# Five counted node tiles instead of six in layer 2 of a two-layer graph network

## The chip, the core and the metric

The kernel runs on one core of a Trainium2 chip. The time is the device time of one execution in microseconds (us); 15 executions of the kernel before have a median of 1412.94 us (1409.12 to 1421.94). Engines: PE (TensorE, matrix products; PEld is its loading of weights), DVE (VectorE), ACT (ScalarE), POOL (GpSimd), SP (SyncE, which only issues transfers here).

## What is computed

A graph has 6250 nodes with 256 features (x) and 100,000 edges src to dst, sorted by dst. The destination is drawn as 6250 u² with u uniform, so nodes with a small number have far more edges than the others. Two layers each add to a node the rows of all its edges' sources and put the sum through two dense products; a residual and a layer norm follow.

```python
def _gin_agg(h, src, dst, eps, n_nodes):
    agg = jax.ops.segment_sum(h[src], dst, num_segments=n_nodes)
    return (1.0 + eps) * h + agg

h = _gin_agg(x, src, dst, eps1, n)
h = jax.nn.relu(h @ W1a + b1a)          # 256 -> 512
h = jax.nn.relu(h @ W1b + b1b)          # 512 -> 512
h = _gin_agg(h, src, dst, eps2, n)
h = jax.nn.relu(h @ W2a + b2a)          # 512 -> 512
out = h @ W2b + b2b                     # 512 -> 256
return _layernorm(x + out)
```

All values are float32.

## The kernel before

**Tiles and chunks.** The nodes lie in 49 tiles of 128 (the last has 106). The edges lie in 782 chunks of 128, in order of dst. There are two ways to sum the rows of the edges:

- *By gathering.* For each chunk, one indirect DMA that GpSimd issues (L270, in `gather`) fetches 128 rows of the table (x, 1 KB a row, in layer 1; h, 2 KB a row, in layer 2) into a buffer called early, in layer 2 early and late. A matmul with a 0/1 matrix `sel` (L1109) adds the rows up within 32 slots. Chunks are taken in groups of 1 to 5 chunks for each of four quarters of the array; at the end of a group the four partial sums are copied and split (L535, L536, L1133), put on their nodes by a matmul with `to` (L1158) and added to the accumulators `acc` of the two or three tiles that the group may reach (L1147).
- *By counts.* For the first, heavily used tiles, layer 1 builds a matrix of how many edges run from each source node to each node of the tile (L939, L942, L985, L955: 280 chunks). The sum is then a product of that matrix with the whole table, tile by tile of the table: 49 matmuls for one node tile in layer 1 (L885 with `both`), 98 in layer 2 (L885 with `upper` and with `xr`, the two halves of a float32 split). For this the table is loaded in 13 ranges of four tiles (`xr`, L823) and split (`cut`, L838). Layer 2 uses the same counts: layer 1 narrows them to 16 bits and stores them (L975, L978), layer 2 loads them (`ci`, L905) and widens them (`cf`, L906). The results are added to acc (L894).

`HEAVY = (7, 6)` (L24) says how many tiles go by counts: seven in layer 1, six in layer 2. `counted` (L65) turns it into the number of leading chunks that lie safely within so many tiles: NC = 280 in layer 1, NC2 = 264 in layer 2. `places` (L100) cuts the chunks beyond into groups, first those from NC2 to NC, then those from NC on; layer 1 takes the groups from `BEGIN` on, layer 2 all of them. So layer 1 gathers 502 chunks in 90 groups, layer 2 gathers 518 in 91.

**Order.** The order of the instructions is written out by the program itself (`manual_schedule`, L560). The main loop (L1093) walks the groups from the last node to the first. Four chunks make a piece; after the matmuls of a piece, the gather of the piece six further on is issued into the same buffer (L1117), so up to 24 chunks are under way:

```python
last_sum[upto] = mm
gathered[upto + PIECES] = gather(number, upto + PIECES, table, width, *places)
for c, b in pieces[number][upto][1]:
    tick()
    for q in both:
        q.pump()
```

With every chunk two queues of other work may put out instructions: `blockwise`, the dense products of those tile pairs whose sums are complete (`block`, L716: transposes L745, copies L754, first product L777, ReLU L786, second product L798, then `finish1` or `finish2`), and `beside`, the products by counts. `spread` (L125) works out how much of `beside` may go with each group, so that it lies where the dense work is thin; its work is proportional to the number of counted tiles (L1072), times a pace of 1.4 in layer 2.

**Blocks.** Tiles are put in pairs (L582 to L585): the counted ones from the front, the others from the back, and the tiles that the very last group reaches in pairs of their own. In layer 2 that makes [0,1], [2,3], [4,5], then [47,48] down to [7,8], and [6] alone at the end: 25 blocks. Each has an accumulator seeded with (1 + eps) times its own rows (L627, L634). Layer 2 begins when layer 1 has stored the last rows of h (L1189). Before its first group it seeds the counted blocks, puts out six steps of `beside`, and then loads the weights W2a and W2b (L511).

**Preparation.** Before either layer, DVE checks that the edges fit the plan (L359 to L491) and writes a flag; each engine branches on it (L1475, L1476). The first 22 gathers of layer 1 are issued ahead of that branch.

Of the kernel before, what the change touches and what calls it, by code (L numbers as in the profile page):

```python
# [20 lines left out]
SLOTS = 32  # L21
BURST = 4
PIECES = 6
HEAVY = (7, 6)  # L24

PASSES = [[6, 5], [4], [3, 2], [1, 0]]
RING = 4
# [37 lines left out]
def counted(N, E, tiles):  # L65

    def node(e):  # L70
        return N * min((e + deviation(e, E)) / E, 1.0) ** 2

    total = 0
    while (
        node((total + PARTS) * P) < tiles * P
        and span(N, E, (total + PARTS) * P, P, SIGMAS) <= W
    ):
        total += PARTS
    taken, at = [], 0
    for n in (8, 4, 2, 1):  # L80
        a = at
        while at + n <= total and span(N, E, (at + n) * P, n * P, SIGMAS) <= W:
            at += n
        if at > a:
            taken.append((a, at, n))
    return total, taken


def steps(N, E, taken, tiles):

    def reached(c):
        return N * min((c * P + deviation(c * P, E)) / E, 1.0) ** 2

    todo = sorted(((c, n) for a, b, n in taken for c in range(a, b, n)), reverse=True)
    return todo, [
        max(i for i, (c, n) in enumerate(todo) if reached(c + n) >= t * P) for t in range(tiles)
    ]


def places(N, E, c, chunks):  # L100

    def node(e, side):
        return N * min(max((e + side * deviation(e, E)) / E, 0.0), 1.0) ** 2

    groups, lo, hi = [], [], []  # L110
    while c < chunks:
        n = min(GRP, -(-(chunks - c) // PARTS) * PARTS)
        while n > PARTS and (
            span(N, E, (c + n) * P, n // PARTS * P, SPREAD, 1) > SLOTS
            or span(N, E, (c + n) * P, n * P, SPREAD, 1) > P
        ):
            n -= PARTS
        groups.append((c, n // PARTS))
        lo.append(int(node(c * P, -1)) // P)
        c += n  # L120
        hi.append(min(int(node(c * P, 1)), N - 1) // P)
    return groups, lo, hi
# [24 lines left out]
def tile_gin_residual_layernorm(  # L147
# [44 lines left out]
    NCH = -(-E // P)  # L192
    NC, taken = counted(N, E, HEAVY[0])
    STEPS, END = steps(N, E, taken, HEAVY[0])

    NC2 = counted(N, E, HEAVY[1])[0]
    assert NC2 <= NC and HEAVY[1] <= HEAVY[0]
    groups, lo, hi = (a + b for a, b in zip(places(N, E, NC2, NC), places(N, E, NC, NCH)))
    NG = len(groups)
    BEGIN = (next(g for g in range(NG) if groups[g][0] == NC), 0)  # L200
    assert lo[BEGIN[0]] >= HEAVY[1]
    NCP = groups[-1][0] + PARTS * groups[-1][1]
# [88 lines left out]
    with tc.tile_pool(name="prep", bufs=2) as prep, tc.tile_pool(  # L291
# [139 lines left out]
        for i in range(2):  # L431
            nc.vector.tensor_tensor(
                diff[:, i, full - NC2 :], diff[:, i, full - NC2 :], real, op=ALU.mult
            )
        bad = prep.tile([P, 8 + HEAVY[0]], F32, tag="bad", name="bad", bufs=1)
        nc.vector.memset(bad, 0.0)
# [1074 lines left out]
```

## Time and profile before

| | |
|---|---|
| median of 15 runs | 1412.94 us |
| the profiled execution | 1412.47 us |
| its span, first to last instruction | 1410.7 us |
| mean granted PE clock | 0.94 of full |
| busy: PE, PEld | 1206.9 us (86%), 724.2 us (51%) |
| busy: DVE, ACT, POOL | 902.2 us (64%), 487.2 us (35%), 1017.0 us (72%) |
| indirect DMAs, layer 1 and layer 2 | 502 and 518 |
| first and last gather issued, layer 1 | 9.67 and 671.37 us |
| first and last gather issued, layer 2 | 704.73 and 1368.86 us |
| HBM read and written | 279.57 MB, 28.83 MB |

A row of busy tenths divides the span into 40 slices of 35.3 us. A timeline row gives start, duration, engine and line, operation, output<-input, how many instructions were merged, and in brackets the idle time before with what ended it. A row of the waits gives the waiting engine and line, what it waited for, us in total, times, and the longest. A matmul in float32 stands in the trace as two records, so "L777 x32" is 16 matmuls of the program. Groups of PE give the time that the group fills and then the mean length of one record; where records overlap, the first is smaller than count times mean.

### The profile page before, as it was taken

What the parts mean: (1) busy time and instruction counts of PE and PEld (TensorE: products, weight loads), DVE (VectorE), ACT (ScalarE), POOL (GpSimd) and SP (SyncE); (2) the same over time, 40 slices, a digit from 0 to 9 for tenths busy, and PEclk for the clock granted to TensorE, in tenths of its full rate; (3) what the DMA queues carried; (4) which work ended last, traced back from release to release, by engine and by line L of the source; (5) the groups of instructions that cost most, each with busy time, mean ns of one, the idle gap of its engine ahead of it and who ended that gap; (6) DMA issues with size and microseconds to landing.
All of it is one profiled execution on the core that took longest, in us unless ns stands there. A gap on an engine that the chain in (4) does not pass through costs nothing. (4 is left out here: it accounts for less than half of the span.)

```text
span 1410.7 us, 18558 instructions
## 1 busy us (share of the span) xinstructions
PE 1206.9 (86%) x5929; PEld 724.2 (51%) x5929; DVE 902.2 (64%) x2267; ACT 487.2 (35%) x892; POOL 1017.0 (72%) x1034
## 2 busy tenths in 40 slices
PE   2589998889897896887845999999989999997977
PEld 1144564445453452553521666676666665663646
DVE  7998778899967667232126577868855654663323
ACT  0223652444344342561314224333423333321112
POOL 6777777777777777777077777777777777777760
PEclk9989999999999899898967899999999999998989
DMA  4645765666466555774398799898889889877761
GB/s 101 199 137 180 240 203 179 199 194 204 144 204 207 170 158 155 220 224 122 108 363 280 205 302 305 263 295 284 256 285 318 292 258 320 267 236 238 222 205 40
DMA packets 159242, 309.77 MB, mean 220 GB/s; under 512 B 25378, under 2 KB 89762, under 8 KB 159136
## 3 DMA queue, kind: packets, MB, share of 16 engines
q0 software_dynamic: 65536, 201.65, 46.5%
q1 hardware_dynamic: 73060, 82.55, 18.2%
q10 hardware_dynamic: 20540, 24.28, 5.1%
q8 instruction: 50, 0.82, 0.2%
q14 instruction: 56, 0.46, 0.1%
HBM read 279.57 MB, written 28.83 MB: 219 GB/s over the span
## 5 line engine op out<-in xcount | busy, mean ns | idle before, releaser
L270 POOL DMA_INDIRECT early<-in_x_dram,srcs x502 | 510.0, 1016 | 159.1 <-issue 132.6
L270 POOL DMA_INDIRECT early<-h,srcs x262 | 257.3, 982 | 112.3 <-issue 64.0
L270 POOL DMA_INDIRECT late<-h,srcs x256 | 247.2, 966 | 80.7 <-issue 64.9
L1147 DVE SCALAR_TENSOR_TENSOR acc<-bank,mask,acc 128x512 f32<-128x512 f32 (+1 forms) x421 | 231.6, 606 | 82.9 <-PE bank L1158 82.7
L1109 PE MATMUL bank<-early,sel 128*32 128x256 f32 (+1 forms) x1528 | 161.6, 499 | 85.8 <-DMA early<-in_x_dram,srcs 36.8
L798 PE MATMUL bank<-w1b_s,ht 128*128 128x512 f32 (+1 forms) x392 | 180.3, 606 | 3.4 <-ACT ht L786 2.9
L777 PE MATMUL bank<-zt,w2a_s 128*128 128x256 f32 (+2 forms) x800 | 181.7, 384 | 1.1 <-ACT zt L754 1.1
L777 PEld LDWEIGHTS bank<-zt,w2a_s 128*128 128x128 f32 x800 | 152.1, 195 | 38.5 <-issue 10.0
L1158 PE MATMUL bank<-split,to 128*128 128x512 f32 (+3 forms) x362 | 122.3, 445 | 25.8 <-ACT split L535 22.8
L885 PE MATMUL bank<-upper,cf 128*128 128x512 f32 (+1 forms) x294 | 125.3, 426 | 12.3 <-ACT cf L906 11.6
L955 DVE TENSOR_TENSOR at<-bank,at 128x490 f32 x173 | 115.0, 665 | 11.0 <-ACT cf L970 3.3
L1109 PEld LDWEIGHTS bank<-early,sel 128*32 128x32 f32 x1528 | 33.6, 112 | 171.0 <-issue 106.9
L798 PEld LDWEIGHTS bank<-w1b_s,ht 128*128 128x128 f32 (+1 forms) x392 | 73.8, 193 | 91.3 <-issue 75.8
L885 PE MATMUL bank<-both,cf 128*128 128x512 f32 (+1 forms) x343 | 111.1, 452 | 10.2 <-ACT ht L786 5.6
L786 ACT ACTIVATE ht<-bank,b2a_s 128x256 f32<-128x256 f32 (+2 forms) x100 | 41.5, 466 | 220.7 <-PE bank L777 216.3
L885 PE MATMUL bank<-xr,cf 128*128 128x512 f32 (+1 forms) x294 | 117.5, 400 | 0.0
L1158 PEld LDWEIGHTS bank<-split,to 128*128 128x128 f32 (+1 forms) x362 | 67.2, 202 | 82.1 <-ACT split L535 34.4
L536 DVE TENSOR_TENSOR both<-xr,both 128x1024 fp32r<-128x1024 f32 (+1 forms) x52 | 60.3, 1159 | 67.3 <-ACT both L535 67.1
L942 DVE TENSOR_SCALAR cb<-numbers,spot 128x490 f16<-128x490 f16 x280 | 103.1, 368 | 0.0
L985 PE MATMUL bank<-cb,ca 128*128 128x490 f16 x280 | 91.3, 395 | 11.7 <-DVE acc L1147 5.4
L654 DVE TENSOR_TENSOR sel<-iota,slot 128x256 f32<-128x256 f32 (+3 forms) x119 | 51.4, 432 | 77.3 <-PE bank L1109 76.4
L777 PE MATMUL bank<-zt,w1a_s 128*128 128x256 f32 (+2 forms) x416 | 96.1, 379 | 3.7 <-DVE at L955 2.6
(132 smaller groups left out, 1556.3 us busy)
## 6 DMA issues: line engine op xcount, KB each, us to landing
xr<-in_x_dram SPq DMA_DIRECT2D x48, 512.0 KB
h<-h1r ACTq DMA_DIRECT2D x48, 256.0 KB
xr<-h SPq DMA_DIRECT2D x12, 1024.0 KB
acc<-h SPq DMA_DIRECT2D x23, 512.0 KB
counts<-ci ACTq DMA_DIRECT2D x72, 128.0 KB
ci<-counts SPq DMA_DIRECT2D x72, 128.0 KB
early<-in_x_dram,srcs POOLq DMA_INDIRECT x502
r<-in_x_dram SPq DMA_DIRECT2D x23, 256.0 KB
```

The lines of the kernel that those rows point to most:

```text
L270: nc.gpsimd.indirect_dma_start(out=rows_[:, j, :], out_offset=None, in_=table, in_offset=bass.IndirectOffsetOnAxis(ap=srcs[:, c : c + 1], ...
L536: nc.vector.tensor_tensor(lower, of, upper, op=ALU.subtract)
L654: nc.vector.tensor_tensor(sel[:, :n, :], iota[:, :SLOTS].unsqueeze(1).to_broadcast([P, n, SLOTS]), slot[:, c0 : c0 + n].unsqueeze(2).to_br ...
L777: nc.tensor.matmul(ph[0][:, (f - o) * TILES * P : (f - o) * TILES * P + nb], wa[:, k, f * P : (f + 1) * P], zt[:, k, :nb], start=(k == 0), ...
L798: nc.tensor.matmul(po[0][:m], ht[:, f, i * P : i * P + m], wb[:, f, :], start=(f == 0), stop=(f == KH - 1),)
L885: nc.tensor.matmul(pm[0], cf[:m, j, :], of.rearrange("p a b -> p (a b)") if once else of, start=(opens and j == 0 and l == 0), stop=(close ...
L942: made = nc.vector.tensor_scalar(b, numbers, spot[:, c : c + 1], None, op0=ALU.is_equal)
L955: nc.vector.tensor_tensor(to, ap.rearrange("p (k w) -> p k w", w=W), to, op=ALU.add)
L985: mm = nc.tensor.matmul(pc[0], a, b, start=(i == 0), stop=(i == n - 1))
L1109: mm = nc.tensor.matmul(pm[b * SLOTS : (b + 1) * SLOTS], sel[:, c - c0, :], rows_[:, j, :], start=(c == parts[b][0]), stop=(c == parts[b][ ...
L1147: nc.vector.scalar_tensor_tensor(acc[t], ap[:, i * width : (i + 1) * width], mask[:, t - lo[g], g : g + 1], acc[t], op0=ALU.mult, op1=ALU.add,
L1158: nc.tensor.matmul(pu[0][:, i * width : (i + 1) * width], to[:used], split[:used, l, :], start=(once or l == 0), stop=(once or l == 1),)
```

## The change

```diff
--- before.py
+++ after.py
@@ -21,7 +21,7 @@
 SLOTS = 32
 BURST = 4
 PIECES = 6
-HEAVY = (7, 6)
+HEAVY = (7, 5)
 
 PASSES = [[6, 5], [4], [3, 2], [1, 0]]
 RING = 4
```

Layer 1 goes on counting seven tiles. It stores the counts of tiles 0 to 4 for layer 2, not those of tile 5 (L973). NC2 becomes 244, and the chunks 244 to 279 make three groups of 16, 16 and 4 chunks where 264 to 279 made one of 16. Layer 2 takes tiles 0 to 4 by counts and gathers 538 chunks in 93 groups; the last group reaches tile 5 alone. Its blocks are [0,1], [2,3], [4], then [47,48] down to [7,8], then [6] and [5], each alone: 26. The instructions of the main path that change in number (program's own instructions, a float32 matmul counted once):

| line | what | before | after |
|---|---|---|---|
| L270 | gathers of h | 518 | 538 |
| L1109 | matmuls on gathered rows, layer 2 | 518 | 538 |
| L1158 | matmuls with to, layer 2 | 182 | 186 |
| L1147 | additions of groups, layer 2 | 211 | 215 |
| L885 | products by counts, layer 2 | 588 | 490 |
| L894, L906, L905 | additions, widened counts, loads of counts, layer 2 | 78 | 65 |
| L975, L978 | narrowed and stored counts, layer 1 | 78 | 65 |
| L777 | first dense product, layer 2: two tiles wide, one tile wide | 368, 16 | 352, 48 |
| L381 to L396 | runs of equal groups in the preparation | 4 | 5 |

## The prediction

> **What bounds the kernel now.** I read four views in this order: the busy share by slice, the waits of each engine in the second layer, the instructions of GpSimd in order of time, and the chain that ended last. First the page: GpSimd's row of 40 slices, and its groups in layer 2.
>
> ```profile
> POOL 6777777777777777777077777777777777777760
> ...
> L270 POOL DMA_INDIRECT early<-h,srcs x262 | 257.3, 982 | 112.3 <-issue 64.0
> L270 POOL DMA_INDIRECT late<-h,srcs x256 | 247.2, 966 | 80.7 <-issue 64.9
> ```
>
> GpSimd shows the same 7 in nearly every slice. It issues one indirect DMA for each chunk of 128 edges, 262 + 256 = 518 of them in layer 2, about 0.97 us each. A steady seven tenths may still be an engine without a break, if the rest is its own pause between instructions. The waits of GpSimd from 700 us on say so:
>
> ```profile
> POOL late L270 <- issue: 64.9, 213, 0.3
> POOL early L270 <- issue: 64.0, 210, 0.3
> POOL early L270 <- DMA h<-h1r: 32.4, 1, 32.4
> ...
> POOL late L270 <- PE bank L1109: 4.8, 7, 3.0
> ```
>
> Columns: idle time in all, how often, longest. 423 idle times are "issue", none over 0.3 us: nothing outside held the engine. It waited 32.4 us once for the last rows of h between the layers, and 3.0 us once for a matmul that had to free a gather buffer. In order of time:
>
> ```profile
> 704.73 0.94 POOL L270 DMA_INDIRECT early<-h,srcs  x1 [32.41 <-DMA h<-h1r]
> ...
> 755.16 0.95 POOL L270 DMA_INDIRECT late<-h,srcs  x1 [3.02 <-PE bank L1109]
> ...
> 1368.86 0.94 POOL L270 DMA_INDIRECT late<-h,srcs  x1 [0.30 <-issue]
> ```
>
> So layer 2 is one unbroken row of gathers from 704.73 to 1368.86 us. TensorE looks as full in the middle, and this row of the busy time by windows is the strongest argument against GpSimd (us, then busy time and count of PE, PEld, DVE, ACT, POOL, then clock, DMA share, GB/s):
>
> ```profile
> 811.90:1235.50 423.60, 415.36 (x2131) 276.40 (x2123) 290.12 (x572) 149.64 (x289) 322.71 (x331) 0.98 0.88 287
> ```
>
> PE is busy 98% there. But had PE set the pace, it would have fallen behind until all 24 gather buffers were full, and GpSimd would have waited for it; in this window it did not, and by 1282 us PE stands waiting for gathers again ("DMA early<-h,srcs" and "late" hold L1109 for 40.3 us in all). The end is then the chain behind the last gathers:
>
> ```profile
> 1363.85 3.75 DMA early<-h,srcs
> ...
> 1367.74 1.07 PE bank L1109 x8
> ...
> 1398.00 3.57 PE bank L777 x32
> 1401.57 1.74 PE bank L798 x8
> ```
>
> **The change, part by part.** HEAVY[1] goes from 6 to 5. By the plan's own arithmetic the counted prefix of layer 2, NC2, falls from 264 chunks to 244, and the instruction lists of the two programs show the rest.
>
> *Twenty more gathers* (518 to 538), two more groups (91 to 93), on the engine that sets the pace. Over the whole layer the spacing is (1368.86 - 704.73 - 2.72)/517 = 1.279 us, the one long wait's excess taken out; the window above gives 423.6/331 = 1.280, and neighbours without any disturbance stand 1.25 apart. I take 20 x 1.28 = **+25.6 us**, ends 25.0 and 25.7 (664.13/517 = 1.285 x 20, the wait left in).
>
> [...]
>
> *One tile's products fewer in layer 2*: 49 + 49 matmuls less of L885.
>
> ```profile
> L885 PE MATMUL bank<-upper,cf 128*128 128x512 f32 x288 | 122.6, 426 | 12.3 <-ACT cf L906 11.6 <-DVE acc L894 0.8
> L885 PE MATMUL bank<-xr,cf 128*128 128x512 f32 x288 | 115.2, 400 | 0.0
> ```
>
> 48 x 0.426 + 48 x 0.400 + two short ones (0.83) = 40.5 us of PE. Added to PE: 20 chunks of L1109, which in layer 2 fill (73.4 + 72.5)/518 = 0.28 us a chunk (columns of the array overlap), 5.6 us; four L1158 at 65.0/180 = 0.36, 1.4 us. A pair of tiles becomes two single ones in the dense part ([4], [6], [5] stand alone where [4,5] and [7,8] with [6] stood): L777 in the chain takes 3.57 us for one tile, 7.17 for two, so about nothing. PE: 40.5 - 7.0 = 33.5 us less. On the path: **0**, because PE is covered by GpSimd's row. Without that cover it would be a gain of 33.5.
>
> *Other engines, layer 2*: ACT loses 13 conversions of counts (12 x 0.62 + 0.30 = 7.7 us), gains 2 x 0.59; DVE loses 13 additions of 0.685 (8.9 us), gains four of 0.74 and two of 0.68 and some masks, about 6. SP loses 13 loads of counts. DVE is busy 405 of the 690 us from 710 on, ACT 209: **0**, the same cover.
>
> *Layer 1*: tile 5's counts are no longer narrowed and stored, 13 casts (7.7 us) and 13 DMA issues on ACT less. The order of PE, SP and GpSimd there is unchanged. ACT is busy 257 of 610 us while gathers run back to back, so **0**; 7.7 us at most if ACT were the bound.
>
> *The preparation*: one more run of groups, some eight small DVE instructions, 1.1 us (the run at 17.36 to 18.5 us shows this sum). It delays the flag (33.62 us), behind which every engine's branch waits. GpSimd has 22 gathers in front of its branch and starts the 23rd at 37.56: 3.9 us of cover, less the branch. **0**; without cover +1.1.
>
> *The start of layer 2*: the 3.0 us wait at 755 comes from the first seeds of acc, which land at 746.66 behind some 3.6 MB of xr and weights; their order in SP's queue is the same but for one load of counts. ACT now has four casts of xr's second range (2.2 us) ahead of the seeds, in a stretch where it stands idle for 27.7 us. **0**, ends -2.7 and +3.
>
> *The tail.* Now: last gather issued at 1368.86, span ends 1410.7, 41.8 us, because the last L1109 stands in PE's order behind dense work that is itself late. In the changed order the last L1109 has one L798 for one tile (1.74) ahead of it, and GpSimd still 5 us to issue its piece, so it waits for its gather: 3.75 to landing (chain, above), 1.07 for its matmuls, then in PE's order L798 1.74, L777 7.17, L1158 0.47, L798 3.46, L745 0.44, the wait for zt 1.12, L777 3.57, L745 0.44, L798 1.74, L777 3.57, L798 1.74 (each from the chain), together 25.5; from the last matmul to the end 1410.7 - 1403.3 = 7.4. Sum 37.7: **-4.1**. But PE will have idled, and after waits of 4.7 and 2.4 us near 1350 an L777 pair took 8.95 instead of 7.07: +1.9. I take **-2.2**, ends -4.1 and +1.
>
> Sum: 25.6 - 2.2 = +23.4. The profiled execution took 1412.47 us (span 1410.7 and 1.8 around it), 0.5 below the median 1412.94. I predict a span of 1434.1 and a median of **1436.3 us**, +1.7%.
>
> **Rivals.**
> 1. *PE sets the pace of layer 2* (other side). For: 98% busy from 812 to 1236. Against: GpSimd's waits. It decides from the point where PE is more than 24 chunks (31 us) behind. Then the 33.5 us of PE go and the gathers hide: 1412.9 - 33.5 = 1379.
> 2. *The bytes set the pace.* For: a DMA share of 0.88 in that window. Against: GpSimd's waits for landings are all 0.6 us or less. 5.24 MB more of h, 1.6 MB less of counts, 3.6 MB at 265 GB/s (710 to 1400 us): +13.7, or 1427.
> 3. *PE, thinned out, runs slow, and the tail grows.* For: granted clock 0.86 and waits for gathers from 1270 to 1370 us, where PE has least to do. If the tail's 33 us of PE work lost a quarter more: 25.6 + 6 or so, 1444.
> 4. *The change does nothing*: excluded by the 20 further gathers in GpSimd's list.
>
> **How the numbers follow.** Forecast 0.83, rival 1 0.03, rival 2 0.05, rival 3 0.07, anything else near the old time 0.02. The forecast's own ends: 25.0 - 4.1 - 2.7 = +18.2 (1431) and 25.7 + 1 + 3 + 1.1 = +30.8, which all the worst cases together need; 1442 leaves out under 2 in 10 with the rivals. Range 1430 to 1442. What can be told from no change is about 0.2%, 2.8 us: faster 0.03, same 0.02, slower 0.95.
>
> **What would show it.** Right: 538 gathers, 1.28 apart, last one issued 25 to 26 us later (1394), "issue" still GpSimd's main idle reason, PE's slices in layer 2 lower, about 38 to 40 us from the last gather to the end. Wrong: a spacing below 1.25; GpSimd's waits on PE gone where there had been many; a last gather before 1390; or a first gather of h away from 704.7 by more than 2 us, which would put the cause in layer 1.

## The result and the profile after

The changed kernel takes 1429.34 us (median of 8 runs, 1425.72 to 1431.45), beside 1412.96 us for the kernel before (40 runs). The ratio is 1.011, 95% interval 1.0095 to 1.0126: slower by 16.4 us. The forecast was 1436.3 us with a range from 1430 to 1442. The direction is right, the size 7 us too large, and the time lies just below the range.

The profiled execution took 1429.64 us with a span of 1427.7. First the page after: GpSimd's row of 40 slices and its groups in layer 2.

```profile
POOL 6777777777777777777077777777777777777770
...
L270 POOL DMA_INDIRECT early<-h,srcs x274 | 262.1, 957 | 115.9 <-issue 69.8
L270 POOL DMA_INDIRECT late<-h,srcs x264 | 255.0, 966 | 80.4 <-issue 67.0
```

There are 538 gathers, and GpSimd still has no idle slice in layer 2. Note the mean of one gather into early: 957 ns where it was 982. Its longest waits from 700 us on (idle time in all, times, longest), and its first and last gather of h in order of time:

```profile
POOL early L270 <- issue: 69.8, 229, 0.3
POOL late L270 <- issue: 67.0, 220, 0.3
POOL early L270 <- DMA h<-h1r: 32.7, 1, 32.7
```

```profile
710.27 0.94 POOL L270 DMA_INDIRECT early<-h,srcs  x1 [32.72 <-DMA h<-h1r]
...
1390.02 0.94 POOL L270 DMA_INDIRECT early<-h,srcs  x1 [0.30 <-issue]
```

Layer 2 starts 5.5 us later than in the first trace of the kernel before, its row of gathers is 679.75 us long instead of 664.13, and the tail behind it 37.7 instead of 41.8. The prediction named a first gather of h more than 2 us away from 704.7 as a sign that the cause lies in layer 1. It came at 710.27 us here, but at 709.14 us in the second trace of the kernel before as well, so the sign tells nothing. One trace of each is a thin base for differences of a few us. This table takes apart every execution profiled, by GpSimd's own instructions in order of time. "Long" is what single gathers took beyond 0.95 us each, "waits" is GpSimd's idle time beyond 0.31 us each, both in layer 2 alone; the columns are us.

| kernel | layer 1, first to last gather | layer 2, first to last gather | gathers | long | waits | last gather to end | span |
|---|---|---|---|---|---|---|---|
| before | 661.7 | 664.1 | 518 | 14.0 | 3.0 | 41.8 | 1410.7 |
| before, again | 666.8 | 664.1 | 518 | 15.3 | 2.1 | 42.3 | 1415.5 |
| changed | 667.1 | 679.8 | 538 | 8.2 | 0.0 | 37.7 | 1427.7 |
| changed, again | 666.4 | 685.5 | 538 | 14.0 | 0.0 | 37.6 | 1432.6 |
| changed, tile 5's counts still stored | 662.2 | 688.2 | 538 | 13.1 | 3.4 | 37.6 | 1430.8 |
| before, tile 5's counts not stored | 664.8 | 659.1 | 518 | 11.9 | 0.6 | 41.9 | 1408.4 |
| before, no subtraction on xr | 667.1 | 654.0 | 518 | 4.3 | 3.1 | 42.5 | 1406.6 |
| changed, no subtraction on xr | 664.5 | 678.6 | 538 | 5.5 | 1.5 | 37.3 | 1424.1 |
| four tiles by counts | 663.3 | 726.3 | 566 | 11.5 | 8.4 | 30.5 | 1463.5 |
| seven tiles by counts | 665.1 | 642.9 | 502 | 8.8 | 7.7 | 49.1 | 1399.8 |
| changed, tiles 5 and 6 in one block | 668.0 | 681.7 | 538 | 10.1 | 0.0 | 41.1 | 1433.5 |
| before, spaced subtractions | 656.5 | 662.1 | 518 | 12.8 | 2.7 | 42.4 | 1403.9 |
| changed, spaced subtractions | 654.5 | 682.2 | 538 | 10.0 | 0.6 | 40.4 | 1420.7 |
| seven tiles, spaced | 655.3 | 650.4 | 502 | 12.0 | 11.9 | 49.4 | 1397.4 |

Layer 2's row less "long" and "waits", divided by the gathers but one, is 1.250 to 1.252 us in all fourteen rows. The two columns take out whatever lies above 0.95 and 0.31 us, so this alone would show little; but the median distance from one gather of layer 2 to the next, nothing taken out, is 1.251 or 1.252 us in every trace, and about nine in ten lie between 1.24 and 1.26. So an undisturbed gather costs 1.25 us in each of these kernels, and everything else in layer 2 is disturbance or tail.

What the disturbance is shows in the first trace of the kernel before in order of time, here GpSimd's and DVE's rows (start, duration, engine, line):

```profile
1114.81 0.95 POOL L270 DMA_INDIRECT early<-h,srcs  x1 [0.30 <-issue]
...
1115.53 2.49 DVE L536 TENSOR_TENSOR xr<-xr,upper 128x512 fp32r<-128x512 f32 x4
...
1116.06 2.79 POOL L270 DMA_INDIRECT early<-h,srcs  x1 [0.30 <-issue]
```

DVE runs four subtractions without a break, 2.49 us, each with both inputs in SBUF. The gather that starts 0.53 us into them takes 2.79 us instead of 0.95 and ends 0.8 us after they do. No list of waits shows that: the gather is longer, not late. In the changed kernel at the same place in time:

```profile
1115.03 0.94 POOL L270 DMA_INDIRECT early<-h,srcs  x1 [0.30 <-issue]
...
1115.10 2.50 DVE L536 TENSOR_TENSOR xr<-xr,upper 128x512 fp32r<-128x512 f32 x4
1116.28 0.95 POOL L270 DMA_INDIRECT early<-h,srcs  x1 [0.30 <-issue]
...
1117.53 0.95 POOL L270 DMA_INDIRECT early<-h,srcs  x1 [0.30 <-issue]
```

It is a burst like the first, but with one gather starting 0.07 us ahead of it and the next 1.18 us into it, and nothing is held up. The Trainium skill has a rule that bears on this: "SBUF — State Buffer", section "Who interferes with whom", says that a DVE instruction with two SBUF inputs contends with a GpSimd instruction that reads SBUF, and that whichever comes first keeps the other out. It also infers that `tensor_tensor`, which this subtraction is, spares the generation of DMA descriptors. The first trace agrees with the rule and not with the exemption: the gather, a DMA, took 2.79 us instead of 0.95. The second, by the times shown, agrees with the rule in neither direction: the gather that came first did not keep DVE out, whose burst ran its usual 2.50 us, and the gather that came during the burst was not kept out either. Twelve bursts of four subtractions and a single one run in layer 2. Charging each long gather to the row of DVE that overlaps it most, they account for 9.1 and 8.5 us of "long" in the two traces of the kernel before, and for 3.4 and 7.7 us in those of the changed one.

### The profile page after: what moved, and what is told of

It reads as the page before. It is cut to its first block, busy times and chain, and to the rows that moved or that the text cites. A ratio compares the mean times of both kernels' runs of the same rounds, so it can differ in the third digit from the quotient of the medians.

```text
span 1427.7 us, 18512 instructions
## 1 busy us (share of the span) xinstructions
PE 1200.5 (84%) x5907; PEld 712.9 (50%) x5907; DVE 898.7 (63%) x2275; ACT 474.8 (33%) x874; POOL 1034.9 (72%) x1054
## 4 chain that ended last, share of the span: by engine, by line
PE 46%; DMA 14%; DVE 14%; POOL 12%; issue 9%; ACT 3%; DVEq 1%; ACTq 1%; SPq 0%; POOLq 0%
PE bank L798 14%; PE bank L777 12%; POOL early L270 8%; PE bank L885 7%; PE bank L1109 7%; DMA late<-h,srcs 5%; POOL late L270 4%; DMA early<-h,srcs 4%; PE bank L1158 4%; DVE at L955 3%; DVE acc L1147 2%; DVE cb L942 2%; DMA acc<-h 2%; PE bank L985 1%; DMA early<-in_x_dram,srcs 1%
## 5 line engine op out<-in xcount | busy, mean ns | idle before, releaser
L270 POOL DMA_INDIRECT early<-in_x_dram,srcs x502 | 515.2, 1026 | 159.1 <-issue 130.4
L270 POOL DMA_INDIRECT early<-h,srcs x274 | 262.1, 957 | 115.9 <-issue 69.8
L270 POOL DMA_INDIRECT late<-h,srcs x264 | 255.0, 966 | 80.4 <-issue 67.0
L1147 DVE SCALAR_TENSOR_TENSOR acc<-bank,mask,acc 128x512 f32<-128x512 f32 (+1 forms) x425 | 234.4, 607 | 65.3 <-PE bank L1158 65.1
L1109 PE MATMUL bank<-early,sel 128*32 128x256 f32 (+1 forms) x1552 | 165.0, 501 | 89.0 <-DMA early<-in_x_dram,srcs 32.6
L798 PE MATMUL bank<-w1b_s,ht 128*128 128x512 f32 (+1 forms) x392 | 183.2, 614 | 3.7 <-ACT ht L786 2.8
L777 PE MATMUL bank<-zt,w2a_s 128*128 128x256 f32 (+2 forms) x832 | 179.1, 372 | 0.7 <-ACT zt L754 0.7
L777 PEld LDWEIGHTS bank<-zt,w2a_s 128*128 128x128 f32 x832 | 150.8, 192 | 38.8 <-issue 12.5
L1158 PE MATMUL bank<-split,to 128*128 128x512 f32 (+3 forms) x366 | 125.3, 450 | 23.7 <-ACT split L535 19.9
L885 PE MATMUL bank<-both,cf 128*128 128x512 f32 (+1 forms) x343 | 111.2, 452 | 13.6 <-ACT ht L786 9.2
L798 PEld LDWEIGHTS bank<-w1b_s,ht 128*128 128x128 f32 (+1 forms) x392 | 75.1, 196 | 93.5 <-issue 78.3
L1109 PEld LDWEIGHTS bank<-early,sel 128*32 128x32 f32 x1552 | 34.0, 112 | 172.7 <-issue 104.2
L885 PE MATMUL bank<-upper,cf 128*128 128x512 f32 (+1 forms) x245 | 105.2, 429 | 12.5 <-DMA ci<-counts 11.9
L1158 PEld LDWEIGHTS bank<-split,to 128*128 128x128 f32 (+1 forms) x366 | 68.7, 205 | 82.2 <-ACT split L535 28.5
L536 DVE TENSOR_TENSOR split<-bank,split 128x512 fp32r<-128x512 f32 (+1 forms) x93 | 62.7, 679 | 64.6 <-ACT split L535 64.6
L1109 PE MATMUL bank<-late,sel 128*32 128x512 f32 x528 | 74.9, 640 | 32.7 <-DMA late<-h,srcs 31.3
L777 PE MATMUL bank<-zt,w1a_s 128*128 128x256 f32 (+2 forms) x416 | 97.1, 382 | 4.4 <-DVE at L955 3.1
```

Of the source, the lines that this page charges most:

```text
L270: nc.gpsimd.indirect_dma_start(out=rows_[:, j, :], out_offset=None, in_=table, in_offset=bass.IndirectOffsetOnAxis(ap=srcs[:, c : c + 1], ...
L536: nc.vector.tensor_tensor(lower, of, upper, op=ALU.subtract)
L777: nc.tensor.matmul(ph[0][:, (f - o) * TILES * P : (f - o) * TILES * P + nb], wa[:, k, f * P : (f + 1) * P], zt[:, k, :nb], start=(k == 0), ...
L798: nc.tensor.matmul(po[0][:m], ht[:, f, i * P : i * P + m], wb[:, f, :], start=(f == 0), stop=(f == KH - 1),)
L885: nc.tensor.matmul(pm[0], cf[:m, j, :], of.rearrange("p a b -> p (a b)") if once else of, start=(opens and j == 0 and l == 0), stop=(close ...
L1109: mm = nc.tensor.matmul(pm[b * SLOTS : (b + 1) * SLOTS], sel[:, c - c0, :], rows_[:, j, :], start=(c == parts[b][0]), stop=(c == parts[b][ ...
```

## The experiments

**The two kernels once more.** There is no edit; these are second traces, and more times for the changed kernel.

> The kernel before once more, for a second trace. Theory 'chance': the time that gathers lose because GpSimd takes longer over single ones (14.0 us in layer 2 and 34.3 us in layer 1 in the first trace) differs by several us from execution to execution of one program. Theory 'phase': it is a property of the program, and comes out within 2 us of 14.0 and 34.3 again, with four gathers of layer 2 over 2 us long; span within 3 us of 1410.7.

Measured: one run, 1417.26 us, span 1415.5. Layer 2's row is 664.1 us again, with 15.3 us of long gathers and four over 2 us. The four are the same gathers in both traces, on the same bursts (774.3, 999.1, 1116.1 and 1147.1 us there, 778.8, 1003.0, 1120.0 and 1151.1 here). Layer 1 took 5.1 us longer, and the span is 4.8 us longer, more than "phase" allows. So layer 2's loss looks like the program's in these two traces, and layer 1's length like chance within 5 us.

> The changed kernel once more. Theory 'phase': layer 1 ends 5 us later than in the kernel before again (last gather of x near 676.6), layer 2 loses about 8 us to long gathers with one over 2 us, the tail from the last gather is 37.7; median +16 us. Theory 'chance': layer 1's length and layer 2's loss move by several us from the first trace of this kernel, the tail stays at 37.7.

Measured: 1430.15 us (6 runs), ratio 1.0116, interval 1.0095 to 1.0137. The tail is 37.6 us, as both theories had it, and layer 1 takes 666.4 us, which fits "phase". But long gathers cost 14.0 us where the first trace had 8.2, three of them over 2 us. So in the changed kernel layer 2's loss moves by 6 us between executions, as in "chance".

**Layer 1's part.** The change drops 13 narrowings and stores from layer 1. One kernel puts them back into the changed one, the other takes them out of the kernel before.

```diff
-                    if t < HEAVY[1]:
+                    if t < HEAVY[1] + 1:
```

(with counts one tile larger), and

```diff
-                    if t < HEAVY[1]:
+                    if t < HEAVY[1] - 1:
...
-                nc.sync.dma_start(ci[:, : len(ks) * P], counts[r, t, :, : len(ks) * P])
+                nc.sync.dma_start(ci[:, : len(ks) * P], counts[r, min(t, HEAVY[1] - 2), :, : len(ks) * P])
```

> The changed kernel, but layer 1 still narrows and stores the counts of tile 5, which nobody reads. If the missing 13 narrowings on ACT are what lengthened layer 1 by 5 us (by moving DVE's work against the gathers), layer 1's gathers take 661 to 663 us again and the time is 4 to 6 us below the changed kernel, about 1424. If layer 1 is longer by chance or through the preparation, no difference within 2 us: 1429.

> The kernel before, but layer 1 does not narrow and store the counts of tile 5, and layer 2 uses those of tile 4 in their place, so tile 5's sums are others. Layer 2's work keeps its size. If the missing narrowings lengthen layer 1, the time is 4 to 6 us above the kernel before, about 1418, with layer 1's gathers at 666 to 668 us; if not, within 2 us of 1413.

Measured: with the stores 1432.23 us (interval of the ratio 1.0112 to 1.0151), beside 1430.15 for the changed kernel in the same session; without them 1411.97 us, ratio 0.9996 (0.9985 to 1.0006). Neither moves the time by the 4 to 6 us of the first theory. Layer 1 took 661.7, 666.8, 662.2 and 667.1 us in the programs that store six tiles' counts in the original spacing, 667.1, 666.4, 664.8, 664.5 and 668.0 in those that store five. The two sets overlap, so the 5 us between the first two traces were chance. The second kernel does as much work in layer 2 as the kernel before, yet lost 11.9 us to long gathers and 0.6 to waits there, not 14.0 to 15.3 and 2 to 3. So the kernel before is not fixed in its loss either.

**The bursts on xr.** DVE's subtraction in layer 2 is left out of both kernels; PE's work and all transfers stay as they are.

```diff
-                        halve(upper[:m, j, :], xr[:m, j, :], whole[:m, j, :])
+                        nc.scalar.copy(upper[:m, j, :], whole[:m, j, :])
```

> The kernel before without DVE's subtraction of the rounded half from xr in layer 2 (49 TENSOR_TENSOR of L536 with both inputs in SBUF, in bursts of up to four); the second half of the split is then the whole row, so layer 2's counted tiles get about twice their sums. Theory 'these bursts hold GpSimd up': no gather of layer 2 over 2 us, long gathers lose 5 us or less instead of 12 to 15, time 7 to 10 us below the kernel before, 1404. Rival 'long gathers come from the memory's side': they stay, 1411 to 1413.

> The changed kernel with the same subtraction left out, and the same effect on the sums. Theory: with the bursts gone from both, the change costs its 20 gathers at 1.2506 us less 4.2 us of tail, 20.8 us above the kernel before without the subtraction; the 16 to 17 us measured with the bursts are smaller only because fewer of them hit gathers. Rival 'the marginal gather is cheaper than its spacing': the difference stays at 16 to 17.

Measured: 1406.90 us (12 runs, ratio 0.9954, 0.9940 to 0.9969) and 1425.88 us (6 runs, ratio 1.009, 1.0069 to 1.0111). GpSimd's groups in the kernel before without the subtraction:

```profile
L270 POOL DMA_INDIRECT early<-h,srcs x262 | 250.2, 955 | 111.9 <-issue 66.4 <-DMA h<-h1r 32.3 <-DMA early<-h,srcs 5.2
L270 POOL DMA_INDIRECT late<-h,srcs x256 | 244.1, 954 | 81.1 <-issue 67.3 <-PE bank L1109 4.6 <-DMA late<-h,srcs 3.7
```

The means of 982 and 966 ns have become 955 and 954, and no gather of either kernel is over 1.41 us: the bursts do hold GpSimd up, and the memory's side is not the cause of the gathers over 2 us. (The edit also takes 31 us of work off DVE. That it is the overlap which counts, and not DVE's load, rests on when the long gathers end; see the last section.) With the bursts the kernel before takes about 6 us more, the changed kernel about 3.5, with an interval from 0 to 5.4. The change without bursts costs 19.0 us (16.8 to 20.9 by resampling the runs); 20.8 was expected, 16 to 17 by the rival. The traces add up to it: 25.0 for the gathers, 5.2 less tail, 0.4 less disturbance, 19.4. But the interval reaches down to the rival's 17, and the gap to the 16.4 with bursts, 2.6 us, has an interval from about 0 to 6, so the times alone do not prove it. What speaks against the rival is the distance of the gathers, 1.25 us in both kernels.

**More and fewer tiles by counts.** HEAVY = (7, 4), and (7, 7); for the latter the assertion on lo goes, and layer 2 also takes gathered edges for counted tiles, `range(lo[g], hi[g] + 1)`.

> Layer 2 takes four tiles by counts and gathers 566 chunks. If GpSimd's row of gathers sets the pace, 28 more than the changed kernel cost 28 x 1.2506 = 35.0 us, time about 1465 with a tail like the changed kernel's. If bytes set it (28 x 256 KB less 1.6 MB of counts, at 265 GB/s), 22 us more: 1452.

> Layer 2 takes seven tiles by counts and gathers 502 chunks; PE gets some 36 us more work. If the row of gathers still sets the pace, 16 fewer are 20 us less: 1393. If PE is so full in layer 2 that it falls 24 chunks behind, GpSimd begins to wait for it (waits on L1109 of 20 us and more in all), the last gather comes no earlier than in the kernel before, and the time is 1405 or more.

Measured: four tiles 1462.23 us (ratio 1.035, 1.0314 to 1.0385), 33 us above the changed kernel. By gathers it should have been 35.0 and by bytes 22. The row itself is 41 and 47 us longer than in the two traces of the changed kernel, 35.0 of it the gathers at 1.25 us and 8.4 a single wait for PE at 764 us; the tail is 7 us shorter. So the gathers set the pace, and the 33 us are a sum in which the tail, which was expected to stay, and the disturbance nearly cancel. Seven tiles 1401.41 us, ratio 0.9924 (0.9896 to 0.9951): faster than the kernel before. Its waits of GpSimd (line numbers are one lower in this kernel, L269 is the gather and L1108 the matmul on its rows):

```profile
POOL late L269 <- issue: 63.1, 207, 0.3
POOL early L269 <- issue: 62.5, 205, 0.3
POOL early L269 <- DMA h<-h1r: 32.1, 1, 32.1
POOL early L269 <- PE bank L1108: 9.1, 6, 3.5
```

16 gathers fewer would be 20.0 us; it gains 12. The last gather comes 18 us earlier than in the kernel before, but the tail grows from 41.8 to 49.1 us. GpSimd's waits beyond 0.31 us are 7.7 us, where the kernel before had 3.0. PE begins to be felt here (busy 422.6 of 423.6 us between 812 and 1236, beside 415.4 before). Both expectations missed in part: it is neither wholly the gathers' time nor PE's.

**The two single blocks at the end.** The changed kernel with tiles 5 and 6 in one block in layer 2.

```diff
-... + pairs(ts) + pairs(tail)
+... + (pairs(ts) + pairs(tail) if number == 1 else pairs(sorted(ts + tail)))
```

> The changed kernel with tiles 5 and 6 in one block at the end of layer 2 instead of two single ones. Theory: the tail is 4.2 us shorter than before because the last L1109 no longer stands behind a late dense block in PE's order; behind it the same records follow either way (25.5 us against 25.5), so the tail stays at 37 to 39 us and the time at 1428 to 1431. Rival 'the two single blocks shorten the tail': it goes back to about 42 us, the time to 1434.

Measured: 1435.44 us (4 runs), ratio 1.0159 (1.0136 to 1.0182), tail 41.1. The theory falls, the rival holds. The chain of the changed kernel from its last gather on (start, us, what):

```profile
1390.02 3.73 DMA early<-h,srcs
...
1393.89 1.07 PE bank L1109 x8
...
1408.23 0.59 ACT zt L754
...
1408.87 3.84 PE bank L777 x32
...
1414.88 3.57 PE bank L777 x32
```

and of this kernel:

```profile
1412.12 0.96 ACT zt L754 x2
...
1413.13 8.86 PE bank L777 x32
1421.99 3.47 PE bank L798 x16
```

Its engines in the 9 us of that product (busy time and count of PE, PEld, DVE, ACT, POOL, then granted clock, DMA share, GB/s):

```profile
1413.00:1422.00 9.00, 8.87 (x33) 7.54 (x34) 0.09 (x1) 0.92 (x3) 0.00 (x0) 0.81 0.09 29
```

Up to L798 the two are alike. With two single blocks the first product for tile 6 starts 1.2 us after the transposes (L745) of its own sums begin, and tile 5's copy runs under tile 6's second product. With one block PE stands idle for 2.1 us while DVE, ACT and then both copies finish, and the product that follows takes 8.86 us instead of 3.84 + 3.57, in 32 records of two tiles instead of 64 of one. The like product of two tiles before the pause took 6.91 us in the same trace. The granted clock was 0.81 during the 8.86 us, and 1.00 from 1397 to 1413 us, during the 6.91 us and the pause. So the product after the pause ran at a lower clock; in the changed kernel the clock was 1.00 in both products of one tile. The 3.4 us between the two tails are most of the 4.4 us by which the changed kernel's tail is shorter.

**Spacing the subtractions.** The result is the same; the subtractions of the lower half in both layers go out one tile per chunk through `later`, the rest before their first matmul. In layer 1 this also cuts each subtraction of four tiles (1.22 us) into four of one tile (0.41 us).

```diff
-                                halve(both[:m, js, 0, :], both[:m, js, 1, :], xr[:m, js, :])
+                                nc.scalar.copy(both[:m, js, 0, :], xr[:m, js, :])
+                        space(of, [...one subtraction for each tile...])
...
+                def space(of, ops):
+                    undone[id(of)] = ops
+                    for k in range(len(ops)):
+                        later(k, lambda: ops and ops.pop(0)())
```

> The kernel before, same result, but the subtractions of the lower half (L536 on xr and both) are put out tile by tile, one per chunk, instead of in one burst. If GpSimd is held up by the length of an unbroken stretch of two-SBUF-input work on DVE, layer 2 loses 5 us or less to long gathers (12 to 15 in one burst) and layer 1 some 10 us less than 34 to 40: time 1396 to 1404. If every such instruction costs a gather the same, no gain: 1411 to 1415.

> The changed kernel with the same spacing. Theory: with the collisions made rare in both, the change costs 20 x 1.2506 - 4.2 = 20.8 us on top of the spaced kernel before, within 2. Rival 'the marginal gather is cheaper than its spacing': 16 to 17.

> Seven tiles by counts in both layers and the spaced subtractions. If the two gains add up, the 12 us of seven tiles and those of the spacing: 1384 to 1392. If PE, fuller with seven tiles, becomes the limit: the last gather waits on L1109 more than the 9 us seen with seven tiles, and the time stays at 1395 to 1401.

Measured: kernel before, spaced, 1404.86 us (ratio 0.9942, 0.9926 to 0.9959); changed, spaced, 1422.28 (1.0066, 1.0049 to 1.0083); seven tiles, spaced, 1399.07 (0.990, 0.9879 to 0.9921), the fastest of all. The first time is a little above the 1396 to 1404 expected. The gain of 8 us is layer 1's, 656 us instead of 662 to 667; whether the cutting or the spacing brought it was not separated. Layer 2 still loses 12.8 us in the spaced kernel before, with three gathers over 2 us, where 5 or less were expected: the 49 subtractions still run in 28 stretches of one to four without a break. The change costs 17.4 us here (16.3 to 18.3), not 20.8, and only just above the rival's 16 to 17. The collisions were not made rare, so this does not decide between the two; the traces give 25.0 for gathers, 2.0 less tail, 4.9 less disturbance, 18.1. Seven tiles and spacing do not add up: GpSimd's waits, now 11.9 us and nearly all on PE, and 12.0 us of long gathers make layer 2's row 7.5 us longer than with seven tiles alone.

## Why the prediction was off

- *What bounds the kernel: right.* Twenty more gathers cost 1.25 us each, on the engine without a break, and the row of gathers with four tiles gives the slope again.
- *Rival 1, PE sets the pace: wrong for this change,* though seven tiles come near it. Its price was wrong as well. The 33.5 us less of PE work counted both groups of L885 in full, but their records overlap: together they fill 158.5 us in layer 2 and not 242.8, and 133.2 in the changed kernel. One tile was worth 25 us, and PE's busy time in layer 2 fell by 8 us only (623.9 to 615.9, means of two traces). This term did not enter the sum.
- *Rival 2, the bytes: its 1427 came closer to 1429 than the forecast did,* but for no good reason. The spacing of gathers did not change with the bytes, and the row with four tiles grew by more than 40 us where the bytes allow 22.
- *Rival 3, a slower PE and a longer tail: wrong.* The tail became shorter, and the product behind the last gather ran at a clock of 1.00.
- *The step that failed is the sum's treatment of disturbance in layer 2's row, which it put at nothing; the tail was mis-sized too.* "The spacing is ... 1.279 us ... I take 20 x 1.28 = +25.6" spread the disturbances evenly over the gathers and let the rest of them stand as they were; "nothing outside held the engine" read that from the idle times alone. The row is 1.25 times the gathers plus single gathers of up to 2.91 us. Twenty gathers are 25.0 us, but the disturbance in layer 2 (long and waits) went from 17.0 and 17.4 us to 8.2 and 14.0: 6 us less by the traces' means, where the sum had 0. Together with the two kernels that differ from these in the counts that layer 1 stores (12.5 and 16.5 us) it is 2.7 us less by the means of three. Even the sum with all its low ends, 1431, lies above the 1429.34 measured.
- *The start of layer 2, taken as 0 with an end of -2.7:* the 3.0 us wait was gone in two traces of the changed kernel and there, 3.4 us, in the one with tile 5's counts stored. It is part of the 6 us above.
- *The tail, -2.2: measured -4.4* (42.1 to 37.6, means of two), 2.2 us of the miss. The addition of PE's records, -4.1, came out, but the reason given for it is only half of it. In the kernel before the last L1109 did stand behind dense work: it starts at 1379.83 us, 11 us after its gather was issued. The kernel with tiles 5 and 6 in one block has this L1109 straight behind its gather, as the changed kernel has, and a tail of 41.1 us all the same. The two single blocks are what shortens the tail. The 1.9 us for a slow clock was not needed, as the first product behind the last gather ran in 6.91 us; with one block that loss was there.
- *Layer 1 and the preparation, 0: upheld*, within 3 us of chance.
- *The sum by two traces each:* 25.0 - 6.1 - 4.4 = 14.5, and 2.8 by which layer 1 and the gap to layer 2 happened to be longer in those traces, 17.3, against 17.1 between the spans and 16.4 between the medians. By the medians, 25.0 - 4.4 = 20.6 leaves 4 us for the disturbance.

What stays open is how much of the lower disturbance belongs to the change, and why. The changed kernel's loss to long gathers varied from 8 to 14 us between two executions, and the kernel before's from 12 to 15 with the one that leaves out tile 5's stores. That the bursts cost time in both kernels is measured; that the difference between the kernels is lasting is not.

## What to carry to other kernels

Where one engine issues without a break, start from the number of its instructions times their undisturbed spacing, read from neighbours and not from the mean over a stage, and price the disturbance and the tail by themselves. Expect less where another engine is nearly full: seven tiles gained 12 of 20 us. Look at the longest instructions of such an engine beside what another engine does at that moment: a hold-up within an instruction was in no list of waits here. When you add up busy time, check whether the records of two groups overlap. And at the end of a kernel, count what PE has ready while a copy is awaited; two small blocks may end sooner than one large one.

## What was not expected of the hardware

In the two traces of the kernel before, seven gathers of 0.95 us took 2.77 to 2.91 us. They started 0.39 to 0.53 us into four two-input DVE subtractions of 2.48 to 2.50 us and ended 0.8 us after them. Others, in the two traces of each kernel, that started 0.3 to 0.55 us into a burst took 0.98 to 1.2 us; those bursts lasted 2.52 to 2.54 us. The ends tell more than the starts. In the nine traces with the bursts in their original form, 77 gathers that started inside a burst of four took over 1.0 us; 22 of them ended 0.81 or 0.82 us after the burst, and the other 55 ended 0.21 or 0.22 us after the end of one of its subtractions. So a gather held up seems to be let in where one subtraction gives way to the next, or after the last. That is argued from the times; what decides which of these gaps it gets was not found. Over layer 1 the 48 larger subtractions of 1.22 us cost gathers 15.4 to 20.0 us in the traces with the original spacing, the largest single loss there.
